# Moving small VectorE work between the matmul phases of a Strassen-Winograd feed-forward block

## The chip, the cores and the metric

The kernel runs on one core of a Trainium2 chip. The metric is device time in microseconds (us), the median of several executions. One further execution was recorded by the hardware profiler; all lines of profile below come from it. The engines are named as the profile names them: PE (TensorE, matmuls), PEld (its weight loads), DVE (VectorE), ACT (ScalarE), POOL (GpSimd) and SP (SyncE, which here only issues DMAs). Each engine works through its own queue in order; semaphores tie the queues together.

## The reference

32 sequences of 128 tokens with 512 features pass through a conditioned block. Its first half (layer norm, two small gelu networks) counts only for masked tokens; its second half is a feed-forward network for all tokens. In a short form:

```python
emb = silu(t) @ ada_w + ada_b                        # shift, scale, gate of the first half
norm = where(m, layernorm(x) * (1 + scale) + shift, 0)
x = x + gate * where(m, ssm(norm) + ssm_of_the_flipped(norm), 0)
shift2, scale2, gate2 = split(silu(t) @ ffada_w + ffada_b, 3)
ff = layernorm(x) * (1 + scale2) + shift2
h = gelu(ff @ ff_w1 + ff_b1)                         # 512 -> 1024
return x + gate2 * (h @ ff_w2 + ff_b2)               # 1024 -> 512
```

## The kernel before

The first 84 us compute the conditioning, the first half for the few masked tokens, and the layer norm of the first eight sequences. The rest, which the change is about, is the feed-forward network. It runs over four **pairs** (p = 0 to 3) of two sides of four sequences each, so 1024 tokens a pair.

**First product.** `ff @ ff_w1` is done with seven block products in place of eight (the Strassen-Winograd scheme), and each of these seven is again cut into seven. The outer seven are called **streams**, and run in the order 1, 2, 5, 6, 3, 7, 4 (`STREAMS`). Each has seven inner products P1 to P7. The text writes 6P3 for product P3 of stream 6. Such a **phase** is four matmuls of 128x128 by 128x256 on line 1117; P5, P2 and P3 add into the PSUM bank that the profile calls `e_m`, P1, P6, P7 and P4 into `a_m`.

After a phase, another engine does something that a later phase of the same stream has to wait for, because the inner sums are formed in PSUM between the matmuls:

- after P1, the **seed**: DVE L1161 `e_m<-a_m,ha` (in streams 1 and 5 an ACT copy, L1163). P2 waits for it.
- after P6, DVE L1142 `e_m<-a_m,...`. P3 waits for it.
- after P7, DVE L1147 `hb<-a_m,...`, which empties the bank. P4 waits for it.
- after P4, DVE L1152 (or ACT L1175). Nothing close waits for it.
- after P5, an ACT copy (L1131), and for streams with a predecessor two POOL additions `with_p5` (L1168), 128x512 each, into SBUF tiles `ha` and `hb`; stream 6 adds three more POOL additions (L1197, `after`), streams 7 and 4 some of L1201 (`late_sum`). L1142 and L1147 read what these leave.

A **window** (function `window`, new stream, old stream) interleaves two streams so that the waits are hidden: new P5, new P1, old P3, old P7, new P2, new P6, old P4. A dictionary `fills[w][n]` says what else is put in after step n of window w; `put(w, n, f, ...)` enters it. Window 1 is streams 2/1, window 2 is 5/2, window 3 is 6/5, window 4 is 3/6, window 5 is 7/3, window 6 is 4/7. All five compute queues stand in the order in which this program text runs (`manual_schedule`); no scheduler reorders them. A step therefore is put in a queue just where the text puts it.

**Sums of x.** The inputs of the streams are sums of blocks of x, made by DVE with `token_sums(j, n)`. j = 1 (L1046) makes the input of stream 5; j = 2 (L1050, tile `xn_sy`) that of stream 6; j = 3 (L1053) that of stream 7; j = 4 (L1056) that of stream 3. n names the part: n = 0 is read by P5 and P6, n = 1 by P1 and P2, n = 2 by P7 and P4 (each 128x512), and n = 3 by P3 (128x256). The text writes sum 4.1 for `token_sums(4, 1)`. Later sums read earlier ones, so their order on DVE is fixed. All their operands lie in SBUF.

**Other fills.** `take_first_half` puts gathers on POOL (L885, `DMA_INDIRECT`), which fetch rows of the first half's result for the next pair. `Statistics.one` is a bn_stats and a bn_aggr on DVE (L917, L918) for one tile of the next pair, `root` the reciprocal square root (L922 on DVE, L923 on POOL). `blocks(side, i)` normalises one such tile (DVE L929) and turns it in 32x32 blocks (DVE STREAM_TRANSPOSE). `fb2_step` is the difference of the two halves of a bias (DVE, 128x256), read by ACT L1243 when a bank of the second product is seeded. `fw2_of.combine` (L394) forms weight sums once, in pair 0.

**Second product.** `h @ ff_w2` follows with one level of the same scheme: 14 steps of 16 matmuls on line 1304. Its first two steps (P1U, P5U) and the third (P1V) stand between the last phases of stream 4; `first_block` (DVE L1251) makes the inputs of P5U and P5V. While it runs, DVE, ACT and DMA queues prepare the next pair, and the last steps are interleaved with stream 1 of the next pair.

Pair 0 is the special one: its first stream starts right behind the first half, so its sums of x come late, and window 1 is written out by hand ahead of the loop.

Of the kernel before, what the change touches and what calls it, by code (L numbers as in the profile page):

```python
# [22 lines left out]
def kernel(  # L23
# [49 lines left out]
    nc = tc.nc  # L73
# [503 lines left out]
    for key, vec in (("ssm1", ssm_b1), ("bwd1", bwd_b1), ("ff1", ff_b1)):  # L577
        n = vec.shape[0] // P
# [823 lines left out]
    now = FirstProduct(0, of_x[0].cut(), of_w)  # L1402
# [17 lines left out]
    for n in range(2, 4):  # L1420
        now.token_sums(1, n)
    now.do(2, "P2", "P6")
    for n in range(4):
        now.token_sums(2, n)
    now.do(1, "P4")
    now.token_sums(3, 0)
    for p in range(NP):
        more_pairs = p + 1 < NP
        xs = x_of[p]
# [2 lines left out]
        def put(w, n, f, *args):  # L1432
            fills.setdefault(w, {}).setdefault(n, []).append(lambda: f(*args))

        if p:
            for n, at in enumerate(((1, 3), (1, 4), (1, 6))):
                put(*at, now.token_sums, 2, 1 + n)
            put(1, 6, now.token_sums, 3, 0)
        for n, at in enumerate(((2, 1), (2, 3), (2, 3))):
            put(*at, now.token_sums, 3, 1 + n)  # L1440
        for n, at in enumerate(((2, 4), (2, 4), (2, 6), (2, 6) if more_pairs else (3, 1))):
            put(*at, now.token_sums, 4, n)
        put(3, 6, now.load_weights, 3)
        if p == 0:
            put(3, 6, load_rows_of_fw2, 0)
# [5 lines left out]
        second = SecondProduct(p, now.h, xs)  # L1451
        if p == 0:
            put(
                2, 0, nc.vector.tensor_tensor,
                fb2_step, fb2[:, D // 2 :], fb2[:, : D // 2], ALU.subtract,
            )
        put(6, 0, now.late_gelu, "11")
# [7 lines left out]
        if more_pairs:  # L1465
            x_next = x_of[p + 1]
            stats = [Statistics(x_next[side], f"{p + 1}_{side}") for side in range(2)]
            xn, xT = {}, {}

            def blocks(side, i):  # L1470

                if i == 0:
                    xn[side] = in_turned_blocks(
                        group_of_tiles(f"{p + 1}_0")
                        if side == 0
                        else sp.tile([P, G, D], F32, tag="s12", name=f"xn_{p + 1}_1")
                    )
                t = stats[side].normalised(i, xn[side][:, :, i])
                nc.vector.transpose(t, t)

            def to_feature_rows(side, *queues):
                xT[side] = new_xT(p + 1, side)
                turned(xn[side], xT[side], queues)

            if p:
                put(1, 6, take_first_half, p + 1, x_next, range(G))
            put(2, 6, take_first_half, p + 1, x_next, range(G, G + 2))
            put(3, 4, take_first_half, p + 1, x_next, range(G + 2, G + 3))
            put(5, 4, take_first_half, p + 1, x_next, range(G + 3, 2 * G))
            for i, at in enumerate(((3, 1), (3, 3), (3, 4), (3, 6))):  # L1490
                put(*at, stats[0].one, i)
            put(*((3, 6) if p else (5, 4)), stats[0].root)
            for i, at in enumerate(((4, 4), (4, 6), (5, 3), (6, 4))):
                put(*at, stats[1].one, i)
            put(6, 4, stats[1].root)
        for w in range(1 + (p == 0), 7):
# [2 lines left out]
        second.step(0)  # L1499
        now.late_gelu("21")  # L1500
        if more_pairs:
            for i in range(2):
                blocks(0, i)
        now.do(4, "P3")
        second.seed(1)
        now.do(4, "P7")
        second.first_block(1, 2, 4)
        if more_pairs:
            blocks(0, 2)
# [16 lines left out]
        if more_pairs:  # L1526

            for i in range(G):
                put(2 + i // 2, blocks, 1, i)
            for k in range(KC):  # L1530
                put(4 + k // 2, lambda k: scaled(2 * (p + 1), xT[0], k), k)
                put(7 + k // 2, lambda k: scaled(2 * (p + 1) + 1, xT[1], k), k)
                if k == 1:
                    put(4, to_feature_rows, 1, nc.sync, nc.sync, nc.sync, nc.scalar)

            def begin(j):
                if j == 1:
                    of_x[p + 1] = TokenBlocks(p + 1, (xT[0], xT[1]))
                of_x[p + 1].one(j)

            put(8, begin, 1)
            put(9, begin, 2)
            put(9, begin, 3)
            put(10, begin, 4)

            def next_product():
                nxt["p"] = FirstProduct(p + 1, of_x[p + 1].cut(), of_w)
                nxt["p"].load_weights(1)

            nxt = {}  # L1550
            put(10, next_product)
            put(11, lambda: nxt["p"].do(1, "P5", "P1"))
            for n in range(4):
                put(11 + n // 2, lambda n: nxt["p"].token_sums(1, n), n)
            put(13, lambda: nxt["p"].token_sums(2, 0))
            if p + 2 < NP:
                x_of[p + 2] = [[], []]
                put(11, lambda: x_of[p + 2][0].extend(load_side(p + 2, 0)))
            put(12, lambda: nxt["p"].do(1, "P2", "P6"))
            put(13, lambda: nxt["p"].load_weights(2))  # L1560
            if p + 2 < NP:
                put(13, lambda: x_of[p + 2][1].extend(load_side(p + 2, 1)))
# [128 lines left out]
```

## Time and profile before

| what | value |
|---|---|
| median of three runs | 456.78 us (456.37 to 456.99) |
| profiled execution, whole / span | 455.45 / 453.7 us |
| granted TensorE clock, mean | 0.999 |
| DVE busy | 331.7 us, 73% of the span |
| ACT, POOL busy | 178.0 and 159.8 us |
| share of PE in the chain that ended last | 92% |
| HBM traffic | 155 GB/s over the span |

The span is what the profiler saw from first to last instruction; the run is 1.7 us longer. In the 40 slices of the page, PE is at 9 tenths or more in every slice but the first and the last, so the profile has to be read at the level of single phases: the start times of neighbouring phases on PE tell where it waited. On an undisturbed stretch the phases of line 1117 start 0.863 us apart.

### The profile page before, as it was taken

The numbers are of one execution on the slowest core, as the hardware profiler recorded it, in microseconds if no ns is written. First come the engines' busy times: TensorE is split into PE (matmuls) and PEld (weight loads), VectorE is DVE, ScalarE is ACT, GpSimd is POOL, SyncE is SP. The second block draws the span as 40 slices with busy tenths as digits, with TensorE's granted clock in tenths as the row PEclk, the third lists the DMA queues.
The fourth block names the chain that finished last, engine by engine and source line by source line (L and its number), as shares of the span: only waits on it lengthen the run. The fifth ranks groups of instructions, "written<-read, shape, count | busy, mean of one in ns | idle before, by whom it ended". The sixth has DMA issues, their size and how long they took to land.

```text
span 453.7 us, 6170 instructions
## 1 busy us (share of the span) xinstructions
PE 446.6 (98%) x2151; PEld 370.4 (82%) x2151; DVE 331.7 (73%) x571; ACT 178.0 (39%) x390; POOL 159.8 (35%) x154
## 2 busy tenths in 40 slices
PE   8999999999999999999999999999999999999996
PEld 3884585688888888888888888888888888888885
DVE  5798797697789759886796498867963995534645
ACT  3124127244642552446425514454355154552000
POOL 4220550089770000797700007977000027560000
PEclk9999999999999999999999999999999999999999
DMA  7999449745518817722187167221872442222023
GB/s 251 379 396 407 150 73 326 279 151 172 189 78 180 114 49 251 249 92 82 66 191 107 56 230 264 95 84 54 202 105 59 157 145 82 81 94 93 0 82 107
DMA packets 82611, 70.57 MB, mean 156 GB/s; under 512 B 63112, under 2 KB 63728, under 8 KB 81554
## 3 DMA queue, kind: packets, MB, share of 16 engines
q1 hardware_dynamic: 67762, 58.28, 40.9%
q0 software_dynamic: 4160, 10.54, 6.9%
q10 hardware_dynamic: 10656, 1.33, 2.1%
q8 instruction: 18, 0.29, 0.2%
q14 instruction: 15, 0.12, 0.1%
HBM read 56.46 MB, written 13.70 MB: 155 GB/s over the span
## 4 chain that ended last, share of the span: by engine, by line
PE 92%; DVE 5%; POOL 1%; issue 1%; ACT 1%; DVEq 0%
PE a_o L1304 23%; PE a_m L1117 18%; PE e_o L1304 18%; PE e_m L1117 14%; PE po_s L221 6%; PE ph_s L204 5%; PE ph_s L673 2%; PE pm_ss L309 1%; PE last L1304 1%; PE pm_f L309 1%; PE a_m_alone L1117 1%; PE pl_s L254 1%; DVE xn_sy L1050 0%; PE part_s L333 0%; DVE e_m L1142 0%
## 5 line engine op out<-in xcount | busy, mean ns | idle before, releaser
L1168 POOL TENSOR_TENSOR ha<-p_m,ha 128x512 f32<-128x512 f32 x20 | 25.8, 1289 | 178.8 <-ACT ha L1175 169.2
L1304 PE MATMUL e_o<-fw,ha 128*128 128x256 f32 x256 | 57.9, 379 | 0.0
L939 ACT ACTIVATE xT<-xT,modT 128x128 f32<-128x128 f32 x112 | 44.1, 480 | 31.6 <-DMA xT<-xn 31.4
L1304 PE MATMUL a_o<-t,hb 128*128 128x256 f32 x240 | 54.1, 379 | 0.0
L1304 PEld LDWEIGHTS e_o<-fw,ha 128*128 128x128 f32 x256 | 48.6, 190 | 6.6
L1304 PEld LDWEIGHTS a_o<-t,hb 128*128 128x128 f32 x240 | 45.6, 190 | 6.2
L1079 ACT ACTIVATE hb<-hb,biasT 128x256 f32<-128x256 f32 x64 | 29.0, 500 | 30.4 <-POOL hb L1201 19.8
L1131 ACT COPY p_m<-e_m 128x512 f32<-128x512 f32 x27 | 15.8, 586 | 47.8 <-PE e_m L1117 43.3
L885 POOL DMA_INDIRECT x<-x_rows,slot_i x24 | 29.2, 1218 | 6.0 <-issue 5.3
L1168 POOL TENSOR_TENSOR hb<-p_m,hb 128x512 f32<-128x512 f32 x20 | 29.6, 1481 | 0.3
L1304 PE MATMUL a_o<-fw,ha 128*128 128x256 f32 x128 | 28.9, 379 | 0.0
L1304 PE MATMUL a_o<-t,s 128*128 128x256 f32 x128 | 28.9, 379 | 0.0
L1304 PE MATMUL e_o<-fw,s 128*128 128x256 f32 x128 | 28.9, 379 | 0.0
L221 PE MATMUL po_s<-w,h_s 128*128 128x512 f32 x64 | 28.4, 594 | 0.0
L1175 ACT COPY ha<-e_m 128x512 f32<-128x512 f32 x32 | 18.5, 578 | 24.9 <-PE e_m L1117 24.6
L1304 PEld LDWEIGHTS a_o<-t,s 128*128 128x128 f32 x128 | 24.3, 190 | 3.3
L1304 PEld LDWEIGHTS a_o<-fw,ha 128*128 128x128 f32 x128 | 24.3, 190 | 3.3
L1304 PEld LDWEIGHTS e_o<-fw,s 128*128 128x128 f32 x128 | 24.3, 190 | 3.3
L1142 DVE TENSOR_TENSOR e_m<-a_m,ha 128x512 f32<-128x512 f32 x20 | 13.9, 696 | 17.0 <-POOL ha L1168 6.6
L1079 ACT ACTIVATE ha<-e_m,biasT 128x256 f32<-128x256 f32 x48 | 20.0, 468 | 14.8 <-PE e_m L1117 12.6
L1117 PE MATMUL a_m<-xT,tw 128*128 128x256 f32 x96 | 24.7, 380 | 0.4 <-DVE hb L1147 0.4
L1117 PE MATMUL e_m<-s,fw 128*128 128x256 f32 x92 | 23.8, 381 | 0.0
(237 smaller groups left out, 892.3 us busy)
## 6 DMA issues: line engine op xcount, KB each, us to landing
tw<-t_rows SPq DMA_DIRECT2D x16, 896.0 KB, 5.3
x<-in_x_dram SPq DMA_DIRECT2D x16, 512.0 KB, 8.8
gate<-gate_rows POOLq DMA_DIRECT2D x8, 1024.0 KB, 5.2
out_dram<-x SPq DMA_DIRECT2D x15, 512.0 KB, 4.9
xT<-xn SPq DMA_DIRECT2D x92, 64.0 KB, 2.4
ada_f<-in_L_cond_ffada_w_dram SPq DMA_DIRECT2D x4, 768.0 KB, 13.2
ada_a<-in_L_cond_ada_w_dram SPq DMA_DIRECT2D x4, 512.0 KB
w<-in_L_cond_ssm_w_dram SPq DMA_DIRECT2D x2, 1024.0 KB, 6.2
```

What stands on the lines that cost most here:

```text
L204: nc.tensor.matmul(ph[:, :n], w[:, k, ts(f, P)], xT[:, k, :], start=(k == 0), stop=(k == KC - 1))
L221: nc.tensor.matmul(po, h[f][:, ts(i, P)], w[:, f, :], start=(f == 0 and seeded is None), stop=(f == HC - 1), skip_group_check=seeded is no ...
L309: nc.tensor.matmul(pm[ts(j, B), : (hi - lo) * P], sT[:, k, :], kinds[:, k, lo:hi, ts(j, P)], start=False, stop=True, skip_group_check=True,)
L885: nc.gpsimd.indirect_dma_start(out=xs[i // G][i % G // 2][:, i % 2], out_offset=None, in_=x1_rows, in_offset=bass.IndirectOffsetOnAxis(ap= ...
L939: nc.scalar.activation(out, src, AF.Identity, bias=shift, scale=scale)
L1079: nc.scalar.activation(dst[:, n], src[:, n], AF.Gelu_apprx_tanh, bias=biasT[:, f : f + 1])
L1117: nc.tensor.matmul(bank[:, ts(n, QT)], self.w_block(j, product)[:, ts(n, P)], self.x_block(j, product), start=(product in ("P1", "P5") and ...
L1131: nc.scalar.copy(p5, e)
L1142: nc.vector.tensor_tensor(e, a, p5, add)
L1168: nc.gpsimd.tensor_tensor(self.place(RESULT[j], c), self.p5[j], other, ALU.add)
L1175: nc.scalar.copy(self.place(RESULT[j], c), src)
L1304: nc.tensor.matmul(part, src[:, k, ts(i, P)], w[product][:, k, :], start=(last and k == 0), stop=True, skip_group_check=True,)
```

## The change

```diff
     now.do(2, "P2", "P6")
-    for n in range(4):
+    for n in range(2):
         now.token_sums(2, n)
     now.do(1, "P4")
-    now.token_sums(3, 0)
     for p in range(NP):
...
+        sums = [(j, n) for j in (2, 3, 4) for n in range(4)]
         if p:
-            for n, at in enumerate(((1, 3), (1, 4), (1, 6))):
-                put(*at, now.token_sums, 2, 1 + n)
-            put(1, 6, now.token_sums, 3, 0)
-        for n, at in enumerate(((2, 1), (2, 3), (2, 3))):
-            put(*at, now.token_sums, 3, 1 + n)
-        for n, at in enumerate(((2, 4), (2, 4), (2, 6), (2, 6) if more_pairs else (3, 1))):
-            put(*at, now.token_sums, 4, n)
+            at_sums = (
+                (1, 1), (1, 3), (1, 4), (1, 6), (1, 6), (2, 1), (2, 3), (2, 3),
+                (2, 4), (2, 4), (2, 6), (2, 6) if more_pairs else (3, 1),
+            )
+        else:
+            sums = sums[2:]
+            at_sums = (
+                (2, 1), (2, 3), (2, 3), (2, 4), (2, 4), (2, 6), (3, 1), (3, 1), (3, 3), (3, 3),
+            )
+        for at, of in zip(at_sums, sums):
+            put(*at, now.token_sums, *of)
...
         if p == 0:
             put(
-                2, 0, nc.vector.tensor_tensor,
+                4, 1, nc.vector.tensor_tensor,
                 fb2_step, fb2[:, D // 2 :], fb2[:, : D // 2], ALU.subtract,
             )
...
-            for i, at in enumerate(((3, 1), (3, 3), (3, 4), (3, 6))):
+            for i, at in enumerate(((3, 1), (3, 3), (3, 4), (4, 1)) if p else ((3, 4), (3, 6), (4, 1), (4, 3))):
                 put(*at, stats[0].one, i)
-            put(*((3, 6) if p else (5, 4)), stats[0].root)
-            for i, at in enumerate(((4, 4), (4, 6), (5, 3), (6, 4))):
+            put(*((4, 1) if p else (5, 4)), stats[0].root)
+            for i, at in enumerate(((4, 4), (5, 1), (5, 3), (6, 4))):
                 put(*at, stats[1].one, i)
             put(6, 4, stats[1].root)
...
         if more_pairs:
-            for i in range(2):
+            for i in range(1 + (p > 0)):
                 blocks(0, i)
         now.do(4, "P3")
         second.seed(1)
         now.do(4, "P7")
+        if more_pairs and p == 0:
+            blocks(0, 1)
         second.first_block(1, 2, 4)
...
             for n in range(4):
                 put(11 + n // 2, lambda n: nxt["p"].token_sums(1, n), n)
-            put(13, lambda: nxt["p"].token_sums(2, 0))
```

No instruction is added or taken away; nothing changes on PE, ACT and SP. On DVE the order changes in these places:

- Pair 0, windows 2 to 4. The last two of the sums 2.n, all of 3.n and 4.n, and `fb2_step` stand later. L1147 of 2P7 now comes ahead of sum 2.3 and the sums 3.n; the sums 4.n stand behind the seed of 6P1, two ahead of and two behind L1147 of 5P7. The first four bn_stats and `fb2_step` follow behind those.
- Pair 0, last phases. L1147 of 4P7 stands ahead of the second normalised tile and its transpose.
- Pairs 1 to 3. Sum 2.0 stands behind the seed of 2P1 and no longer ahead of it.
- Pairs 1 and 2. The fourth bn_stats and its root stand behind the seed of 3P1, another bn_stats behind the seed of 7P1 (the latter in pair 0 too).

On POOL, the reciprocal root of side 0 in pairs 1 and 2 moves behind the two L1168 of stream 3.

## The prediction

> **What bounds the kernel now.** I read the busy shares first:
>
> ```profile
> PE 446.6 (98%) x2151; PEld 370.4 (82%) x2151; DVE 331.7 (73%) x571; ACT 178.0 (39%) x390; POOL 159.8 (35%) x154
> ```
>
> PE sets the time, so a move on DVE is worth only the PE wait that it ends or makes. Next the timeline of PE. An undisturbed phase starts 0.863 us after the one before it (100.83 after 99.97 below).
>
> ```profile
> 97.75 1.03 PE L1117 MATMUL a_m<-sx,tw 128*128 128x256 f32 x4
> 99.00 1.13 PE L1117 MATMUL a_m<-xT,t 128*128 128x256 f32 x4 [0.23 <-DVE hb L1147]
> 99.97 1.03 PE L1117 MATMUL e_m<-xn_sy,tw 128*128 128x256 f32 x4
> 100.83 1.03 PE L1117 MATMUL a_m<-xn_sy,tw 128*128 128x256 f32 x4
> 101.75 1.13 PE L1117 MATMUL e_m<-sx,tw 128*128 128x256 f32 x4
> 102.72 1.03 PE L1117 MATMUL a_m<-sx,tw 128*128 128x256 f32 x4
> 103.88 1.13 PE L1117 MATMUL e_m<-xn_sy,tw 128*128 128x256 f32 x4
> 104.85 1.03 PE L1117 MATMUL a_m<-xn_sy,tw 128*128 128x256 f32 x4
> ...
> 129.89 3.62 PE L1304 MATMUL e_o<-fw,s 128*128 128x256 f32 x16
> 133.93 1.13 PE L1117 MATMUL a_m<-xT,tw 128*128 128x256 f32 x4 [0.42 <-DVE hb L1147]
> ```
>
> These are 5P6, 2P4 (99.00), 6P5, 6P1, 5P3 (101.75), 5P7, 6P2 (103.88), 6P6; then P5U and 4P4. A phase that had to wait costs its lateness plus 0.10, since the next starts 0.97 later and not 0.86. 2P4: 1.25 - 0.86 + 0.10 = 0.50. 5P3: 0.05 + 0.10 = 0.16. 6P2: 0.30 + 0.10 = 0.41. 4P4: 16 matmuls take 3.45, so 134.04 less 0.10 was due at 133.34; 0.59 + 0.10 = 0.69. Read the same way, 7P2 waits in pairs 1 and 2 (207.63, 298.58; 0.28 each) and 2P2 in pair 3 (365.35; 0.29). All these are 2.61 us. The rest of the network has next to no gap.
>
> Last, POOL and DVE, to see what stands in each other's way:
>
> ```profile
> 90.84 1.26 POOL L1168 TENSOR_TENSOR ha<-p_m,ha 128x512 f32<-128x512 f32 x1 [27.17 <-ACT ha L1175]
> 92.08 1.71 POOL L1168 TENSOR_TENSOR hb<-p_m,hb 128x512 f32<-128x512 f32 x1
> ...
> 98.59 1.00 POOL L885 DMA_INDIRECT x<-x_rows,slot_i  x1 [0.31 <-issue]
> 99.89 2.07 POOL L885 DMA_INDIRECT x<-x_rows,slot_i  x1 [0.30 <-issue]
> 102.26 1.83 POOL L885 DMA_INDIRECT x<-x_rows,slot_i  x1 [0.30 <-issue]
> 104.11 1.28 POOL L1168 TENSOR_TENSOR ha<-p_m,ha 128x512 f32<-128x512 f32 x1
> ```
>
> ```profile
> 91.65 1.01 DVE L1046 TENSOR_TENSOR sx<-xT 128x512 f32<-128x512 f32 x1
> 92.58 1.48 DVE L1046 TENSOR_TENSOR sx<-s 128x256 f32<-128x256 f32 x1
> ...
> 102.81 0.41 DVE L1056 TENSOR_TENSOR s<-s,xn_sy 128x256 f32<-128x256 f32 x1
> 103.14 0.68 DVE L1161 TENSOR_TENSOR e_m<-a_m,ha 128x512 f32<-128x512 f32 x1
> ```
>
> A sum whose operands all lie in SBUF and a POOL addition don't run together. The sum of 91.65 (0.68 elsewhere) ends at 92.66, 0.55 after the addition; the next addition ends 1.13 after that sum, at 93.79; the 256-wide sum, 0.41 elsewhere, ends 0.28 later still. So they alternate: the waiting addition goes ahead of the next sum. At 184.5, 275.4 and 366.4 the same rows show the same ends to 0.01. L1142, L1147, L1161 (PSUM operands) and bn_stats overlap additions with no loss. The point: before, the last sum ends at 103.2, ahead of the first addition of stream 6 at 104.11.
>
> **What goes.** 2P4's wait: L1147 loses sums 2.3, 3.0, `fb2_step` and 3.1 ahead of it and starts when 2P7 ends (97.15, from 98.27). 5P3 and 6P2 start on time too: L1142 of 5P6 ends at 100.6 for a need at 101.2, the seed of 6P1 at 102.15 for 102.93. That is 1.07. 4P4: L1147 moves ahead of the second tile, whose 1.27 (131.28) is 0.74 of waiting for POOL's addition; it ends some 1.4 before 4P4 is due: 0.69. L1147 then fills that wait, so the last `first_block` behind it, which ended at 138.02, ends about 0.5 earlier; P5V, due at 138.51 and now 0.69 earlier, still has it by 0.3. 7P2 in pairs 1 and 2: its seed sat behind a bn_stats and bn_aggr (0.81), which now follow: 0.56. The root moved on POOL costs nothing: it still stands ahead of the addition L1197 that L1142 of 3P6 waits for (204.84), so that wait stays. Sum 2.0 behind the seed, pair 3: 0.60 off the seed, 0.29 won; in pairs 1 and 2 PE had no wait there. `fb2_step` (0.34) is read by ACT at 122.3, late enough. All edits: -2.61.
>
> **What comes.** I queue the changed order of pair 0 by the durations above (sums 0.60 start to start, 256-wide 0.335, bn pair 0.81, DVE starts 0.10 after a phase's last matmul, which ends 1.03 after its start).
> - DVE: 2.3 at 97.75, 3.0, 3.1, 3.2, L1142 99.89, L1152, 3.3 at 101.09, seed 6P1 101.47, 4.0 at 102.07, 4.1 due 102.67.
> - POOL's gathers: the one of 97.07 now meets no sum (1.00, was 1.21); the next starts 98.38 in sum 3.0 (till 98.69, 1.27), the next 99.95 (1.00, was 2.07), the last 101.26 in 3.3 (1.14). Stream 6's first addition comes at 102.40 instead of 104.11, in the middle of sum 4.0.
> - So 4.0 ends 102.75, addition 103.87, 4.1 104.42, L1147 of 5P7 104.34 to 105.03 (due 103.27). 5P4, due 104.66, starts at 105.09: 0.43 + 0.10.
> - Second addition 105.55, sum 4.2 106.10, third (L1197) 107.22, sum 4.3 107.50, bn 107.42 to 108.24, L1142 of 6P6 to 108.93. 6P3, due 107.79 after the first delay, starts 108.99: 1.20 + 0.10.
> - `fb2_step` meets the additions of stream 3 and ends 111.2; bn; L1147 of 6P7 111.9 to 112.6; 6P4 due 112.55: 0.10 + 0.10. From there DVE is ahead again, POOL's later additions (1.3 later) still end before L1142 of 7P6, which ACT holds.
>
> New: 0.53 + 1.30 + 0.20 = 2.03, call it 2.04. Sum: 2.04 - 2.61 = -0.57, a span of 453.16 from 453.73. The profiled execution is 455.45 in all, the median of the runs 1.33 more; the difference carries over: **456.2**.
>
> Bounds of what the trace doesn't show, which is who wins where a gather waits for a sum: it let a second sum pass twice in ten such rows (99.89, 102.26, both beginning under 0.1 into the sum), never when it began later. Mine begin 0.29 and 0.17 into one. If one slips by 0.6, the addition comes at 103.0, 4.1 is through, and the new waits are 6P3 0.77 and 6P4 0.36: sum -1.5. Delayed by 1.2: 6P3 0.30 and 3P3 0.50, sum -1.8. I take the row that holds for later beginnings.
>
> [...]
>
> **Rivals.**
> 1. The additions miss the sums, or only touch them: the gathers slip as bounded above, or POOL lets queued sums pass. For it: two gathers did slip. Against: in all six rows where an addition waits and more DVE work on SBUF is queued (92.08, 184.48, 219.12, 275.44, 310.08, 366.39), the addition went first. 455.3 with one slip, 454.9 with two, 454.2 with no new wait at all (-2.61).
> 2. Slower: POOL becomes the bound of pair 0. It idles no more than 0.3 at a time from 90.84 to 117.89, and every meeting adds up to 0.6. If seven sums cost it 0.6 each, the addition for 7P6 ends at 116.66 + 4.2 = 120.9, where L1142 has to start by 118.6 to keep 7P3: 2.3 + 0.1 more. 2.04 + 2.4 - 2.61 = +1.8: 458.6. It decides from an end at about 119.5, half a microsecond past what ACT's copies allow with my delays. Against it: queued as above, POOL is 1.3 late.
> 3. The change doesn't do what it says: each L1147 and seed named does move ahead in the changed order, so only sizes are open.
>
> **Chances.** Forecast (meeting as queued, or its near variants) 0.60, rival 1 0.33, rival 2 0.07. 0.2% is 0.91 us, about what a measurement can tell: faster means below 455.87. The forecast's own range, 455.7 to 456.7, crosses that line, about 0.05 of its 0.60. So faster 0.38, same 0.55, slower 0.07. Range: the forecast's, down to rival 1's two slips and some room, 454.7; up 0.3 over the forecast's, 457.0; outside are no new wait and rival 2.
>
> **What will show it.** Right: 2P4, 4P4, the three seeds with no gap; the gather of 99.9 near 1.0; stream 6's first L1168 near 102.4; sums 4.1 and 4.3 stretched to 1.7 and 1.5; gaps before 5P4 and 6P3. Wrong: sums 4.n at 0.68 and no gap in pair 0 (rival 1), or L1142 of 7P6 waiting for POOL L1168 (rival 2).

## The result, and the profile after

The changed kernel takes 460.08 us (median of ten runs, 456.63 to 461.15) against 456.40 for the kernel before (ten runs, 455.51 to 457.21): a ratio of 1.0075 [1.0054, 1.0097]. It is slower by 3.7 us, where 456.2, or 0.57 less than before, was forecast and "slower" had a chance of 0.07. Nine of the ten runs lie between 459.1 and 461.2; the one of 456.63 has a span of 454.9 and the higher clock (0.999); no trace of it is on record, so why it was spared is not known.

The profiled execution has a span of 459.4, from 453.7. The page's busy shares and its row of granted clock (40 slices):

```profile
PE 448.9 (98%) x2151; PEld 372.4 (81%) x2151; DVE 338.8 (74%) x571; ACT 178.2 (39%) x390; POOL 159.5 (35%) x154
```

```profile
PEclk9999999998999999999999999999999999999998
```

PE is busy for 2.3 us more with the same matmuls, and two slices have a clock below 0.9: the tenth, 103 to 115 us, and the last, where PE's matmuls have ended (455.0). The timeline of PE in the tenth, with the same phases as shown before:

```profile
98.13 1.03 PE L1117 MATMUL a_m<-sx,tw 128*128 128x256 f32 x4
99.00 1.03 PE L1117 MATMUL a_m<-xT,t 128*128 128x256 f32 x4
...
101.59 1.03 PE L1117 MATMUL e_m<-sx,tw 128*128 128x256 f32 x4
...
103.31 1.03 PE L1117 MATMUL e_m<-xn_sy,tw 128*128 128x256 f32 x4
104.18 1.03 PE L1117 MATMUL a_m<-xn_sy,tw 128*128 128x256 f32 x4
108.32 1.55 PE L1117 MATMUL a_m<-sx,tw 128*128 128x256 f32 x4 [3.12 <-DVE hb L1147]
109.67 1.91 PE L1117 MATMUL e_m<-s,fw 128*128 128x256 f32 x4
111.37 1.49 PE L1117 MATMUL a_m<-xT,fw 128*128 128x256 f32 x4
112.70 1.03 PE L1117 MATMUL e_m<-xn_sy,tw 128*128 128x256 f32 x4
...
116.56 1.13 PE L1117 MATMUL a_m<-xn_sy,tw 128*128 128x256 f32 x4 [0.25 <-DVE hb L1147]
```

2P4 (99.00), 5P3 (101.59) and 6P2 (103.31) start 0.86 after the phase ahead of them: these waits are gone. But 5P4 starts 4.14 after 6P6 and not 0.86 after it, and the three phases from 108.32 to 112.70 take 4.38 and not 2.59. What 5P4 waited for stands on DVE and POOL:

```profile
102.47 4.60 DVE L1056 TENSOR_TENSOR s<-s,xn_sy 128x512 f32<-128x512 f32 x1
106.99 0.68 DVE L1056 TENSOR_TENSOR xT<-xT,xn_sy 128x512 f32<-128x512 f32 x1
107.59 0.68 DVE L1147 TENSOR_TENSOR hb<-a_m,p_m 128x512 f32<-128x512 f32 x1
```

```profile
101.65 1.12 POOL L885 DMA_INDIRECT x<-x_rows,slot_i  x1 [0.30 <-ACT p_m L1131]
102.80 1.28 POOL L1168 TENSOR_TENSOR ha<-p_m,ha 128x512 f32<-128x512 f32 x1
104.02 1.27 POOL L1168 TENSOR_TENSOR hb<-p_m,hb 128x512 f32<-128x512 f32 x1
105.24 1.26 POOL L1197 TENSOR_TENSOR ha<-ha 128x512 f32<-128x512 f32 x1
106.66 1.30 POOL L885 DMA_INDIRECT x<-x_rows,slot_i  x1 [0.16 <-issue]
```

Sum 4.0, 0.68 elsewhere, is recorded for 4.60: it comes 0.33 before the first addition of stream 6, and waits not for one addition but for all three, which run undelayed at 1.26 to 1.28. It ends at 107.07, 0.57 after the last of them. Sum 4.1 and L1147 of 5P7 follow, and 5P4 with them.

The windows view of the same stretch (time, then busy time of PE, PEld, DVE, ACT and POOL, the granted clock, the DMA's share and GB/s):

```profile
104.00:108.30 4.30, 1.20 (x6) 0.72 (x4) 4.30 (x4) 0.59 (x1) 3.80 (x4) 1.00 0.00 0
108.30:110.00 1.70, 1.68 (x5) 1.45 (x6) 1.67 (x5) 0.09 (x1) 0.00 (x0) 0.68 0.08 20
110.00:112.50 2.50, 2.50 (x8) 1.94 (x8) 1.42 (x4) 1.08 (x2) 0.15 (x1) 0.54 0.64 181
```

PE did next to nothing for 3.1 us. It then ran some 3.4 us at half the clock: the granted clock is 0.50 all through 109.0 to 112.2 and 1.00 again from 112.4 (the 0.68 and 0.54 above are means that take in some full speed), and matmuls start 0.427 apart and not 0.216. The half clock adds 1.79 to the 3.28 by which 5P4 is late.

The balance, read by the distances between phase starts as the prediction reads them: 5P4 3.28; the halved clock behind it 1.79; 6P4 0.51; P1V, behind 4P4, 0.37; the fourth products of stream 6 in pairs 1 and 2 0.23 each; pair 3's 2P2 and 2P3 0.41; 7P5 in pair 3 1.03. Together 7.85, less the 2.61 of the old waits: +5.24. The two spans differ by 5.64 (459.37 and 453.73), of which 0.39 lies before 84 us, where nothing was moved.

### The profile page after: what moved, and what is told of

Same layout as the page of the kernel before. It is cut to its first block, busy times and chain, and to the rows that moved or that the text cites. A ratio compares the mean times of both kernels' runs of the same rounds, so it can differ in the third digit from the quotient of the medians.

```text
span 459.4 us, 6170 instructions
## 1 busy us (share of the span) xinstructions
PE 448.9 (98%) x2151; PEld 372.4 (81%) x2151; DVE 338.8 (74%) x571; ACT 178.2 (39%) x390; POOL 159.5 (35%) x154
## 3 DMA queue, kind: packets, MB, share of 16 engines
q10 hardware_dynamic: 10656, 1.33, 2.1%
## 4 chain that ended last, share of the span: by engine, by line
PE 91%; DVE 3%; issue 2%; POOL 2%; DMA 1%; ACT 1%; DVEq 0%
PE a_o L1304 23%; PE a_m L1117 18%; PE e_o L1304 17%; PE e_m L1117 14%; PE po_s L221 6%; PE ph_s L204 5%; PE ph_s L673 2%; DMA tw<-t_rows 1%; PE pm_ss L309 1%; PE last L1304 1%; PE a_m_alone L1117 1%; PE pm_f L309 1%; PE part_s L333 1%; POOL hb L1201 1%; PE pl_s L254 1%
## 5 line engine op out<-in xcount | busy, mean ns | idle before, releaser
L1168 POOL TENSOR_TENSOR ha<-p_m,ha 128x512 f32<-128x512 f32 x20 | 26.3, 1315 | 183.6 <-ACT ha L1175 169.3
L885 POOL DMA_INDIRECT x<-x_rows,slot_i x24 | 27.8, 1159 | 6.0 <-issue 5.0
L1168 POOL TENSOR_TENSOR hb<-p_m,hb 128x512 f32<-128x512 f32 x20 | 29.6, 1482 | 0.3
```

The costliest lines, as they stand in the source:

```text
L885: nc.gpsimd.indirect_dma_start(out=xs[i // G][i % G // 2][:, i % 2], out_offset=None, in_=x1_rows, in_offset=bass.IndirectOffsetOnAxis(ap= ...
L1168: nc.gpsimd.tensor_tensor(self.place(RESULT[j], c), self.p5[j], other, ALU.add)
```

## The experiments

Times are beside the kernel before on the same chip (medians 456.1 to 456.4). A time marked "one execution" has no spread and shows little by itself, since executions of the kernel before on one chip spread over 1.6 to 3.9 us; what such a run shows is its trace. A **row** of additions means POOL additions that follow each other at once; a sum that waits for such additions is called shut out. Notation as in the prediction; the numbers on spans and waits are from each run's own trace.

**1. Is the wait there again?** The changed kernel, unaltered.

> The changed kernel once more, unaltered. In its first profile DVE sum 4.0 of pair 0 took 4.60 us (0.68 elsewhere): it was dispatched in the tail of POOL's last gather, and three POOL additions ran ahead of it, none of them delayed. Theory S (starved): a sum dispatched in a gather with additions queued right behind it gets no turn until POOL's queue has a pause; the stretch of 3.5 to 4.6 and the wait of some 3 us before phase 5P4 come again in this profile. Rival A (they alternate, as I forecast, and the first profile was an accident): the sum takes about 1.0 and the wait is 0.4. Time: S 460, A 456.

460.86 (459.19 to 460.98), ratio 1.0087 [1.0054, 1.0121]. Sum 4.0 takes 4.59, over three additions of 1.26 to 1.28; 5P4 starts 3.27 late, and the clock is 0.50 from 106.9 to 113.6. So it isn't an accident of one execution.

**2. Where in the change does the loss sit?** Pair 0's sums, `fb2_step` and the first four statistics at the places of before; the rest stays changed.

```diff
-    for n in range(2):
+    for n in range(4):
         now.token_sums(2, n)
     now.do(1, "P4")
+    now.token_sums(3, 0)
...
-            sums = sums[2:]
+            sums = sums[5:]
             at_sums = (
-                (2, 1), (2, 3), (2, 3), (2, 4), (2, 4), (2, 6), (3, 1), (3, 1), (3, 3), (3, 3),
+                (2, 1), (2, 3), (2, 3), (2, 4), (2, 4), (2, 6), (2, 6),
...
-                4, 1, nc.vector.tensor_tensor,
+                2, 0, nc.vector.tensor_tensor,
...
-            for i, at in enumerate(((3, 1), (3, 3), (3, 4), (4, 1)) if p else ((3, 4), (3, 6), (4, 1), (4, 3))):
+            for i, at in enumerate(((3, 1), (3, 3), (3, 4), (4, 1)) if p else ((3, 1), (3, 3), (3, 4), (3, 6))):
```

> The changed kernel with pair 0's sums, its bias step and its first four bn_stats at their old places; the tile behind 4P7 and all edits of pairs 1 to 3 stay. Both theories: the sums run before the additions again, the old waits before 2P4, 5P3 and 6P2 (1.07) come back, none near 5P4, clock 1.00; 4P4's 0.69 stays won. Against the kernel before 0.7 to 1.2 us less (455.2 to 455.7), which puts the whole loss of the change on the place of these sums. If it stays near 460, the loss is elsewhere.

455.71, ratio 0.9990 [0.9973, 1.0007]. The three old waits are back (2P4, 5P3 and 6P2, 0.50, 0.15 and 0.41 by the same reading), the loss is gone. So the whole loss comes from the place of pair 0's sums and of what was moved with them (`fb2_step`, four statistics), and all other parts together are worth 0.1%, within what can be told from no change.

**3. Sums 4.0 and 4.1 two phases later.** A sum that doesn't start in the tail of a gather.

```diff
-                (2, 1), (2, 3), (2, 3), (2, 4), (2, 4), (2, 6), (3, 1), (3, 1), (3, 3), (3, 3),
+                (2, 1), (2, 3), (2, 3), (2, 4), (2, 4), (2, 6), (3, 3), (3, 3), (3, 3), (3, 3),
```

> The changed kernel with sums 4.0 and 4.1 of pair 0 put behind L1147 of 5P7 with 4.2 and 4.3. Gathers as in the changed kernel, but sum 4.0 is now dispatched about 1.3 us later, in the second addition. S: the four sums alternate with the additions, no sum over 1.8 us; 5P4 has no wait, 3P5 and 3P1 wait some 1 us in all for 4.0 and 4.1. Rival B: sum 4.0 is shut out until the third addition ends, 2.5 us or more. Rival D: 4.6.

456.92 (one execution). Sum 4.0 comes 0.10 into the second addition and takes 2.95: it waits for the second and the third and gets in when POOL comes to its gather. So the tail of the gather isn't needed for it. PE waits twice, 1.3 and 1.1; the mean clock of the span is 1.000.

**4. The last two gathers ahead of the additions left out in pair 0.** This run leaves out part of the work: two tiles of the next pair miss their first-half rows.

```diff
-            put(2, 6, take_first_half, p + 1, x_next, range(G, G + 2))
+            if p:
+                put(2, 6, take_first_half, p + 1, x_next, range(G, G + 2))
```

> The changed kernel without the two gathers that stand in POOL's queue ahead of stream 6's additions in pair 0 (two tiles of the next pair then miss the first half's rows for masked tokens). The additions then start as soon as ACT's copy is there, about 101.2, and sum 4.0 is dispatched at 102.1 in the middle of the first addition, with no gather near. S: it waits for one addition only, as the sums of stream 5 do, and takes about 1.0 to 1.3; the following sums alternate; PE's waits before 5P4 and 6P3 together are under 2 us and the clock stays at 1.00. Rival B (whatever the gathers do, three additions in a row shut a sum out): sum 4.0 takes 3 us or more. Rival D (it is the sum itself, not POOL): 4.6 again.

457.21 (one execution). POOL now rests 1.62 ahead of the first addition. Its timeline, and DVE's:

```profile
100.72 1.38 POOL L1168 TENSOR_TENSOR ha<-p_m,ha 128x512 f32<-128x512 f32 x1 [1.62 <-ACT p_m L1131]
102.06 1.72 POOL L1168 TENSOR_TENSOR hb<-p_m,hb 128x512 f32<-128x512 f32 x1
104.10 1.35 POOL L1197 TENSOR_TENSOR ha<-ha 128x512 f32<-128x512 f32 x1 [0.33 <-ACT ha L1175]
```

```profile
101.53 1.12 DVE L1056 TENSOR_TENSOR s<-s,xn_sy 128x512 f32<-128x512 f32 x1
102.57 1.75 DVE L1056 TENSOR_TENSOR xT<-xT,xn_sy 128x512 f32<-128x512 f32 x1
```

Here sums and additions do alternate: sum 4.0 gets in after one addition, the second addition is stretched to 1.72, sum 4.1 to 1.75. This is the picture that the prediction drew for the change. The waits left on PE are 0.9 and less. A little later `fb2_step`, begun 0.16 into the second addition of stream 3, also gets in after one, though POOL had rested only 0.84 ahead of that row:

```profile
107.74 1.26 POOL L1168 TENSOR_TENSOR ha<-p_m,ha 128x512 f32<-128x512 f32 x1 [0.84 <-ACT p_m L1131]
108.96 1.26 POOL L1168 TENSOR_TENSOR hb<-p_m,hb 128x512 f32<-128x512 f32 x1
110.19 1.45 POOL L1197 TENSOR_TENSOR ha<-ha 128x512 f32<-128x512 f32 x1
```

```profile
109.12 1.39 DVE L1432 TENSOR_TENSOR fb_step<-fb 128x256 f32<-128x256 f32 x1
```

**5. A gather ahead of the additions instead of behind them.** The additions start later, so another sum meets them.

```diff
-            put(3, 4, take_first_half, p + 1, x_next, range(G + 2, G + 3))
+            put(*((3, 4) if p else (2, 6)), take_first_half, p + 1, x_next, range(G + 2, G + 3))
```

> After the runs so far: a sum dispatched 0.1 into the second addition, more than a us after the gather's end, was shut out by two additions (2.95), while without the two gathers sums and additions alternated (1.12, 1.75). Theory S2: after a gather, as long as POOL goes on without a pause, a sum gets no turn until POOL pauses. Rival A2 (only a sum dispatched before or right at the start of an addition loses). Here the gather of step (3, 4) of pair 0 stands with the others at (2, 6), so the additions come some 1.3 later, at 103.7, right behind the last gather; sums 4.0 and 4.1 meet gatherings only and take 0.7 to 1.3. Sum 4.2, dispatched about 103.9: S2, it waits for all three additions, 3.3 to 4.0; A2, if it is dispatched before 103.8 the same, else one addition, 1.7. Time in both near 457; with S2 phase 6P3 waits 1.5 or more.

459.99 (one execution). Sums 4.0 and 4.1 pass in 0.68 and 0.74; sum 4.2, started 0.23 into the first of the additions, takes 4.05 while three of them run at 1.27 or 1.28. 6P3 comes 3.65 late, and the clock is 0.995 over the span. So it isn't sum 4.0 or its place: here it is sum 4.2 that meets the row. The row does not end there, though: a fourth addition follows without a rest, and this one waits for the sum.

```profile
106.58 1.27 POOL L1197 TENSOR_TENSOR ha<-ha 128x512 f32<-128x512 f32 x1
107.81 1.73 POOL L1168 TENSOR_TENSOR ha<-p_m,ha 128x512 f32<-128x512 f32 x1
```

**6. A short rest of POOL.** A one-element operation on POOL that waits for ACT's copy after 5P3 stands ahead of the three additions.

```diff
-                if prior and j not in (2, 4):
+                if prior and j not in (2, 4) and not (self.p == 0 and j == 6):
...
+            pause = stp.tile([1, 1], F32, tag="pause", name="pause", bufs=1)
+            put(
+                3, 2, nc.gpsimd.tensor_scalar,
+                pause, now.place("22", "12")[0:1, 0, 0:1], 1.0, None, ALU.add,
+            )
+            put(3, 2, now.with_p5, 6, "12")
+            put(3, 2, now.with_p5, 6, "22")
```

> The changed kernel with a pause in POOL's queue between the last gather and stream 6's additions in pair 0: a one-element POOL operation there reads ACT's copy after 5P3, which ends at about 102.9, and the two additions follow it; POOL idles from 102.4 to then. Sums 4.0 and 4.1 run in the pause, sums 4.2 and 4.3 (dispatched 103.9 on) meet additions. S2: the pause has ended POOL's hold, so sums and additions alternate: no sum over 1.8, some addition stretched to 1.4 to 1.8. Rival B2 (additions that stand close shut sums out whatever came before): sum 4.2 takes 2.5 or more and no addition is stretched. PE: no wait before 5P4 over 0.3; time 455 to 456 with S2.

456.80 (one execution). POOL rests 0.56, does the small operation, and adds; DVE's sum 4.2 is shut out by three again (104.05 3.82):

```profile
103.11 0.51 POOL L1432 TENSOR_SCALAR pause<-ha 1x1 f32<-1x1 f32 x1 [0.56 <-ACT ha L1175]
103.60 1.26 POOL L1168 TENSOR_TENSOR ha<-p_m,ha 128x512 f32<-128x512 f32 x1
104.83 1.26 POOL L1168 TENSOR_TENSOR hb<-p_m,hb 128x512 f32<-128x512 f32 x1
```

No gather stands directly ahead of the row, and the sum is shut out all the same. The clock makes a difference, too: 6P3 starts 2.29 late here and the clock stays at 1.00, and the total is 3 us under that of the changed kernel, for a wait that is 1.0 shorter (one execution, and not the only wait that differs).

**7. Sums earlier, the gather moved, the root in pairs 1 and 2 later.** A first attempt at a better version.

```diff
-                (2, 1), (2, 3), (2, 3), (2, 4), (2, 4), (2, 6), (3, 1), (3, 1), (3, 3), (3, 3),
+                (2, 1), (2, 1), (2, 1), (2, 3), (2, 3), (2, 4), (2, 4), (2, 6), (3, 1), (3, 1),
...
-            put(3, 4, take_first_half, p + 1, x_next, range(G + 2, G + 3))
+            put(*((3, 4) if p else (2, 6)), take_first_half, p + 1, x_next, range(G + 2, G + 3))
...
-            put(*((4, 1) if p else (5, 4)), stats[0].root)
+            put(5, 4, stats[0].root)
```

> A version that keeps what was won and avoids the meeting. Pair 0: sums 2.2, 2.3 and 3.0 in the gap ahead of L1147 of 2P7, 3.1 and 3.2 behind it, 3.3 and 4.0 ahead of L1142 of 5P6, 4.1 behind L1152 of 2P4, 4.2 and 4.3 behind the seed of 6P1; the gather of step (3, 4) stands at (2, 6), so that additions begin after about 103.4. The root of side 0 is put at (5, 4) in all pairs, so that its small DVE operation (1.09 in an addition in pair 1, ahead of L1147 of 6P7) is not ahead of a wait. All theories: no sum meets an addition, no PE wait over 0.2 in pair 0 before 4P4, where ACT's bank seed keeps some 0.4; in pairs 1 and 2 the waits before 6P4 (0.23) go. Against the kernel before 1.5 to 2.1 us less, 454.3 to 454.9.

458.52, ratio 1.0048 [1.0032, 1.0064]: a miss. The sums are through by 103.5, but a gather beside them takes 2.44, the additions start at 105.72, and six of them run in a row to 113.1. Now `fb2_step` meets them: 110.07, 3.30, shut out by three, 6P4 2.77 late, the clock halved again (0.994 over the span). The waits of pairs 1 and 2, however, are gone with the root's new place.

**8. A long rest of POOL.** The two L1168 of stream 6 are held back behind L1197, which waits for ACT's copy after 6P2; sums 4.2 and 4.3 stand behind a one-element operation of DVE that waits for the same copy.

```diff
-                if prior and j not in (2, 4):
+                if prior and j not in (2, 4) and not (self.p == 0 and j == 6):
...
-                (2, 1), (2, 3), (2, 3), (2, 4), (2, 4), (2, 6), (3, 1), (3, 1), (3, 3), (3, 3),
+                (2, 1), (2, 3), (2, 3), (2, 4), (2, 4), (2, 6), (3, 1), (3, 1), (3, 4), (3, 4),
...
+            late = stp.tile([1, 1], F32, tag="late", name="late", bufs=1)
+            put(
+                3, 4, nc.vector.tensor_scalar,
+                late, now.place("21", "11")[0:1, 0, 0:1], 1.0, None, ALU.add,
+            )
+            put(3, 4, now.with_p5, 6, "12")
+            put(3, 4, now.with_p5, 6, "22")
```

> The changed kernel with the three additions of stream 6 in pair 0 held back: the two L1168 are issued in 6P2 (behind L1197 of quarter 11, which waits for ACT's copy after 6P2, so POOL should be idle some 1.5 to 2.5 us behind the gathers), sums 4.2 and 4.3 stand in 6P2 too, behind a one-element DVE operation that waits for the same copy. So sum 4.2 is dispatched 0.1 to 0.5 into the first of three additions that could follow each other at once. Theory I (POOL's history decides: after a rest of 1.6 us or more a sum is let in after one addition, behind a run of gathers it is not): sum 4.2 takes 1.4 to 1.8, the addition after it is stretched to 1.6 to 1.8, no PE wait above 2. Theory D (the moment of dispatch decides: earlier than some 0.7 us into an undelayed addition means shut out until POOL stops adding): sum 4.2 takes 3.5 to 4.2, the three additions take 1.26 to 1.29 each, and PE waits over 2 us for 6P3 with a halved clock behind it. Total 457 to 458 by I, 459 to 460.5 by D.

460.25 (one execution). It did not test what it was made for: DVE got in first. What it showed, on POOL and on DVE:

```profile
104.20 2.16 POOL L1197 TENSOR_TENSOR ha<-ha 128x512 f32<-128x512 f32 x1 [2.28 <-ACT ha L1175]
...
110.00 1.28 POOL L1168 TENSOR_TENSOR ha<-p_m,ha 128x512 f32<-128x512 f32 x1
111.22 1.27 POOL L1168 TENSOR_TENSOR hb<-p_m,hb 128x512 f32<-128x512 f32 x1
112.45 1.27 POOL L1197 TENSOR_TENSOR ha<-ha 128x512 f32<-128x512 f32 x1
```

```profile
104.22 0.67 DVE L1056 TENSOR_TENSOR xT<-xT,xn_sy 128x512 f32<-128x512 f32 x1
104.81 0.41 DVE L1056 TENSOR_TENSOR s<-s,xn_sy 128x256 f32<-128x256 f32 x1
...
109.62 4.38 DVE L1432 TENSOR_TENSOR fb_step<-fb 128x256 f32<-128x256 f32 x1
```

Sum 4.2 starts 0.02 after L1197 and runs in 0.67; sum 4.3 follows it at once, and the addition, 1.27 elsewhere, waits for both (2.16). So two sums in a row can keep an addition out, as a row of additions keeps a sum out. Six microseconds later the roles are turned: `fb2_step`, 0.41 elsewhere, comes in the tail of a gather, 0.38 before the first of three additions, and takes 4.38. 6P4 waits 3.39 and starts at 115.47; the clock is 1.00 to 116.7 and 0.50 from 116.9 to 120.1. It is the failure of the changed kernel at another place, with another operand and half the width.

**9. The old places, and the root of pairs 1 and 2 later.** Experiment 2, and one line more.

```diff
-            put(*((4, 1) if p else (5, 4)), stats[0].root)
+            put(5, 4, stats[0].root)
```

> Pair 0's sums, the step of fb2 and the first four statistics at the places of before, the rest as changed, and L921/L922 (root and rstd) of pairs 1 and 2 four windows later at (5, 4), as pair 0 has them. Theory: the new waits before 6P4 of pairs 1 and 2 (0.12 and 0.10 behind it, twice) go and the old ones of 7P2 do not come back; with pair 3's as in sums_back 455.2 (454.6 to 455.7), ratio 0.997 or 0.998, no PE start over 0.30 us after the one before between 150 and 360. Rival: the root only moves its wait to another product, 455.7 and a ratio of 0.999.

455.24, ratio 0.9978 [0.9958, 0.9998]. No start on PE between 150 and 360 us is more than 0.24 after the one before: both the old wait before 7P2 and the new one before 6P4 are gone.

**10. Pair 0's sums forward instead of back.** In the kernel before DVE stands idle from 86.2 to 88.2 and from 89.0 to 89.7.

```diff
-    for n in range(2):
+    for n in range(4):
         now.token_sums(1, n)
+    now.token_sums(2, 0)
+    nc.vector.tensor_tensor(fb2_step, fb2[:, D // 2 :], fb2[:, : D // 2], ALU.subtract)
...
     now.do(2, "P5")
+    now.token_sums(2, 1)
     now.seed(2)
...
-    for n in range(2, 4):
-        now.token_sums(1, n)
     now.do(2, "P2", "P6")
-    for n in range(2):
+    for n in range(2, 4):
         now.token_sums(2, n)
     now.do(1, "P4")
+    now.token_sums(3, 0)
...
-            sums = sums[2:]
+            sums = sums[5:]
...
-                (2, 1), (2, 3), (2, 3), (2, 4), (2, 4), (2, 6), (3, 1), (3, 1), (3, 3), (3, 3),
+                (2, 1), (2, 3), (2, 3), (2, 4), (2, 4), (2, 6), (2, 6),
```

The statistics and the root are as in experiment 9, and the old `put` of `fb2_step` is gone.

> A version made from the findings: pair 0's sums go forward instead of back. Sums 1.2, 1.3, 2.0 and the step of fb2 in DVE's idle 86.1 to 88.1, sum 2.1 in the idle 88.8 to 89.5, 2.2 and 2.3 behind 2P6, the rest at the places of before; the statistics of pair 0 as before, the later ones spread as in the change; L921/L922 of every pair in 6P1's window after next (5, 4). Theory: DVE's queue runs 1 to 1.5 us ahead of before at 94 to 104, no addition meets a sum that waits, so the waits of 2P4 0.50, 5P3 0.16 and 6P2 0.41 are gone or under 0.1 each, with no wait above 0.5 in 104 to 120: 454.1 (453.3 to 455.0), ratio 0.995. Rival P (POOL bounds this stretch: six gathers, then three additions, cannot start earlier): L1142 of 6P6 or 3P6 waits for POOL what was won, 455.0, as v3. Rival S (a sum is shut out by two or three additions at another place): over 457 with a gap of 2.5 us or more.

455.16, ratio 0.9976 [0.9959, 0.9993]: no better than experiment 9, and short of the forecast. The waits of 2P4 and 5P3 are gone, but the gathers come earlier too, the first addition stands at 101.28, and the last sum, 4.3, meets it (1.49 for 0.41). The seed of 6P1 behind it is late, 6P2 loses 0.93 and 0.10.

**11. No sum left to meet.** Experiment 10 with the sums 3.2 to 4.3 one step further forward.

```diff
-                (2, 1), (2, 3), (2, 3), (2, 4), (2, 4), (2, 6), (2, 6),
+                (2, 1), (2, 1), (2, 1), (2, 3), (2, 3), (2, 4), (2, 4),
```

> v2_sums_in_idle with its sums 3.2 and 3.3 put where DVE stood idle (95.7 to 97.1, in 2P7's place the window before) and sums 4.0 to 4.3 one or two products earlier, so that all of pair 0's sums are done by 100 and none is left when the first addition of stream 6 starts at about 101.5. Theory (the meeting of a sum with an addition is all that is left to pay in this stretch): sum 4.3, which waited there for one addition (1.49 instead of 0.41) and held the seed L1161 and PE back (1.144 between two starts at 103.55, 0.93 and 0.10 lost), takes 0.41; no PE start over 0.30 us after the one before between 90 and 130; the three additions of stream 6 take 1.26 to 1.33; 454.1 (453.3 to 454.9), ratio 0.995 or 0.996. Rival: the sums press on the six gathers instead (2.0 or more for one, as in v1), the additions start after 103 and L1142 of 6P6 waits for POOL: 455.2, as v2, with a gap of 0.5 or more near 106.

454.12 (452.85 to 455.19), ratio 0.9953 [0.9935, 0.9971]; the span is 451.8. This beats both kernels. The row of additions starts with no sum near it (the last ends at 99.45):

```profile
101.64 1.28 POOL L1168 TENSOR_TENSOR ha<-p_m,ha 128x512 f32<-128x512 f32 x1
102.87 1.28 POOL L1168 TENSOR_TENSOR hb<-p_m,hb 128x512 f32<-128x512 f32 x1
104.12 1.27 POOL L1197 TENSOR_TENSOR ha<-ha 128x512 f32<-128x512 f32 x1
```

No start on PE between 90 and 130 us comes more than 0.24 after the one before.

**12. One sum back into the row.** Experiment 11 with the last sum, 4.3 (128x256), behind the seed of 6P1.

```diff
-                (2, 1), (2, 1), (2, 1), (2, 3), (2, 3), (2, 4), (2, 4),
+                (2, 1), (2, 1), (2, 1), (2, 3), (2, 3), (2, 4), (3, 1),
```

> v2b_no_meeting with a single sum moved by three products: 4.3 (128x256) from 5P2 to behind the seed of 6P1. DVE reaches it at about 101.6, POOL then ends its sixth gather and starts the first of three additions at 101.5 to 101.7 without a rest and without having waited for a sum. Theory (such an addition and those behind it keep the sum out; it gets in when POOL stops adding): sum 4.3 takes 3.8 to 4.4, the three additions 1.26 to 1.33 each, L1147 of 5P7 ends some 3.5 later than in v2b, PE waits 3 or more for 5P4 and its clock halves behind that: 458 to 459.5, ratio to before 1.004 to 1.008, for one sum of 0.41. Rival (as I forecast for the change: the sum waits for one addition only): 4.3 takes 1.4 to 1.6, the second addition 1.4 to 1.7, 5P4 late by 1 or less, 455 to 455.4.

455.57, ratio 0.9994 [0.9978, 1.0010]: 1.4 us more than experiment 11 (the spans are 453.2 and 451.8). On DVE, POOL and PE:

```profile
101.88 2.65 DVE L1056 TENSOR_TENSOR s<-s,xn_sy 128x256 f32<-128x256 f32 x1
```

```profile
101.75 1.27 POOL L1168 TENSOR_TENSOR ha<-p_m,ha 128x512 f32<-128x512 f32 x1
102.97 1.26 POOL L1168 TENSOR_TENSOR hb<-p_m,hb 128x512 f32<-128x512 f32 x1
104.45 1.27 POOL L1197 TENSOR_TENSOR ha<-ha 128x512 f32<-128x512 f32 x1 [0.21 <-ACT ha L1175]
```

```profile
105.98 1.13 PE L1117 MATMUL a_m<-sx,tw 128*128 128x256 f32 x4 [1.37 <-DVE hb L1147]
```

The mechanism is as expected and the size is not (458 to 459.5 was expected; the time of the rival, 455 to 455.4, is nearer): both L1168 run undelayed past the waiting sum, but L1197 then waits 0.21 for ACT, and in that gap the sum gets in. As it is shut out by two and not by three, 5P4 waits 1.37, and the phases behind it start 0.97 and 0.86 apart, as at the full clock. One sum of 0.41, moved by three products, takes back 1.4 of the 2.1 that experiment 11 had won. Read by phase starts, 5P4 costs 1.64; the spans differ by 1.43, because 0.33 more lies before 84 us and the wait of 7P5 in pair 3 (below) is 0.54 shorter here.

**The meetings together.** The table has sums and `fb2_step` against rows of additions. "Ahead" is what POOL did before the row of additions; the start is the sum's, against the addition that it meets.

| Sum (experiment) | Ahead of the row | Start | Additions waited for | Took, us |
|---|---|---|---|---|
| 4.0 (changed kernel) | gather, no rest | 0.33 before the first | 3 | 4.60 |
| 4.0 (3) | gather, no rest | 0.10 into the second | 2 | 2.95 |
| 4.2 (5) | gather, no rest | 0.23 into the first | 3, then a fourth waits for it | 4.05 |
| 4.2 (6) | rest 0.56, small operation | 0.45 into the first | 3 | 3.82 |
| `fb2_step` (7) | gather, then three additions | 0.68 into the fourth | 3 | 3.30 |
| `fb2_step` (8) | gather, no rest | 0.38 before the first | 3 | 4.38 |
| 4.3 (12) | gather, no rest | 0.13 into the first | 2, then POOL rests 0.21 | 2.65 |
| 1.2 (before) | rest 27.17 | 0.81 into the first | 1 | 1.01 |
| 4.0 (4) | rest 1.62 | 0.81 into the first | 1 | 1.12 |
| `fb2_step` (changed kernel) | rest 4.39 | 0.04 into the second | 1 | 1.50 |
| `fb2_step` (4) | rest 0.84 | 0.16 into the second | 1 | 1.39 |
| 4.3 (10) | gather, but the first addition itself waited for a sum (1.33) | 0.11 into the first | 1 | 1.49 |

A sum got in after one addition where POOL had rested for 0.84 us or more ahead of the row, or where that addition had itself waited for a sum. Where the row came straight behind other work, or behind a rest of 0.56 and a small operation, it stayed out for two or three additions. It then got in mostly where POOL rested or went over to a gather, but in experiment 5 ahead of a fourth addition, so it need not wait for the whole row. The moment of the start does not order the rows: 0.04 and 0.16 into an undelayed addition got in after one, 0.68 did not. The nearest to a matched pair is sum 4.3 in experiments 10 and 12, at 0.11 and 0.13 into the first addition. So what POOL did before orders the table; what decides it inside the chip is not shown by any of these runs, and the one made for it (8) did not reach its case.

## Why the prediction was wrong

**What goes** held in part. 2P4, 5P3 and 6P2 start on time, 1.06 where 1.07 was forecast. 4P4's wait goes too, but of the 0.69 only 0.32 is kept, for P1V behind it waits for its weights, and those for a bank that ACT seeds:

```profile
138.74 0.59 ACT L1243 COPY a_o<-fb 128x512 f32<-128x512 f32 x1
```

```profile
139.38 1.59 PEld L1304 LDWEIGHTS a_o<-fw,ha 128*128 128x128 f32 x8 [0.51 <-ACT a_o L1243]
```

The step named DVE's work behind 4P4 and forgot ACT's queue. 7P2 in pairs 1 and 2 starts on time, but "the root moved costs nothing" is wrong: its L922, 0.34 before, now stands ahead of L1147 of 6P7, starts inside an addition and takes 1.09. That gives back 0.23 of 0.28, twice; experiment 9 shows that a later place has neither wait. In pair 3 the 0.29 is lost again at 2P2 and 2P3 (0.17 and 0.24): sum 2.0, behind the seed, now meets the L1168 of 369.65, which takes 1.74.

**What comes: the gathers** held to 0.02. They take 1.00, 1.26, 1.00 and 1.12 where 1.00, 1.27, 1.00 and 1.14 were queued, and the first L1168 of stream 6 stands at 102.80, or 102.41 without the 0.39 of the start, where 102.40 was queued. Gathers begun inside a sum mostly took longer than the 1.00 of one that met none: 1.26 inside sum 3.0 here, 2.44 in experiment 7, 2.07 and 1.83 in the trace of before. One in experiment 5, begun 0.01 into sum 4.1, took 1.00, and that sum 0.74.

**What comes: the meeting** is the step that failed: "So 4.0 ends 102.75, addition 103.87, 4.1 104.42". Sum 4.0 was taken to be in ahead of the addition, and every later sum to wait for one addition. Sum 4.0 waited for three. The rows that "they alternate" was read from (91.65 and its three like) all stand behind a POOL that had rested 27 us or more; the row in question stands behind six gathers. The trace of before had no meeting of that sort, and the text named as unknown only who wins between a gather and a sum. The bound for a sum against a row of additions was missing: one addition on the one side, the whole row, 3 x 1.23, on the other. With it, rival 2 would have had a place and a price: 5P4 late by 3.3 instead of 0.43. Why sum 4.0, which starts 0.33 ahead of the first addition, is passed by it stays open.

**The clock** is the other half, and was in no rival. Of the 5.07 lost at 103 to 113 us, 1.79 is the halved clock. PE stood idle for 3.12 here, 3.11 in experiment 1, 2.61 in 7, 3.39 in 8 and 3.49 in 5, and in each of these five traces a stretch at a granted clock of 0.50 came with it: of some 3.4 us in four of them, and of 6.8 in experiment 1. Behind 2.13 (6), 1.42 (8), 1.37 (12) and 1.15 (3) the clock stayed at 1.00. The stretch does not begin at a fixed distance from the wait: in experiment 1 the clock is 0.50 from 106.9, ahead of 5P4's start at 107.50, in 8 it falls more than 1.2 after 6P4's start. Behind PE's last matmul, where nothing is left to slow down, it falls some 2.1 after the matmul's end in the changed kernel (457.1) and some 3.1 in the kernel before (452.5). Of the executions without a trace, one of three in experiment 1 and five of seven in experiment 7 have a mean clock of 0.998 or more, against 0.991 to 0.995 in the others; what PE waited in them is not recorded. In these traces waits of 2.61 and more between phases came with a halved clock and those of 2.13 and less did not; where the bound lies, and whether a wait of 2.13 at another moment would have come with one, no run shows.

**Rivals.** Rival 1 (the additions miss the sums) did not happen in the changed kernel, but its price was right for a kernel in which it does: with no new wait it put 454.2, and experiment 11, where no sum meets the row, gave 454.12. That they agree so closely is in part luck: rival 1 took 2.61 from 456.78, experiment 11 is 2.09 under the 456.21 beside it, and it also has the root at a later place and 0.86 of waiting at 7P5 in pair 3. Rival 2 (slower, 458.6) had the sign and a size 1.5 short, by a mechanism that did not occur: POOL was not late through many small meetings, since the three additions of stream 6 lost nothing. Forecast 6P3 1.30 and 6P4 0.20: 6P3 has no wait, since 5P4's delay covers it, and 6P4 has 0.51.

That the loss comes from the sums' place is shown by experiment 2; that a wait for several additions makes it, by experiments 5, 8, 11 and 12.

## What to carry to other kernels

Where operations of two engines hold each other up, as the sums and the additions do here (0.68 for a 512-wide sum alone, 1.01 to 4.60 in a meeting), a wait seen once is a sample of one history: price a new meeting from one operation up to the row that stands behind it on the other engine (three additions were the most that a sum waited for here), and look at what that engine did just before. Work that nothing waits for belongs into idle time ahead of such a row, not behind it: the same sums, with what was moved beside them, cost 4.4 us moved back (460.08 against 455.71 in experiment 2) and won 1.1 moved forward until none met the row (454.12 against 455.24 in experiment 9). And a wait on PE can have two prices: in the traces of these runs a stretch at half the clock came with every wait between phases of 2.6 us or more, and in the changed kernel it cost 1.79.

## What else the runs showed

In pair 3, 7P5 waits for its weights from DRAM (L1063) in ten of the thirteen traces of changed kernels, and not in the kernel before. Its start is late by 0.96 in the changed kernel, 1.07 in experiment 1, 0.72 in 3, 0.52 in 6, 1.15 in 7, 0.96 in 10, 0.78 in 11, and 0.14 to 0.28 in 4, 5 and 12 (0.07 to 0.08 more is lost behind it, hence the 1.03 of the balance); it isn't late in 2, 8 and 9. The transfer is issued at the same point each time. What differs in the records is one 16 KB packet near it, of the queue kind that the profile calls instruction: it took 0.92 to 0.93 in before, 2 and 9, and 1.5 to 2.4 in the ten that wait, though also 2.0 in experiment 8, which does not. There may be a link; no run was made for it.

A small DVE operation can wait as well: L922, on 128x4 elements, took 1.09 inside an addition in pairs 1 and 2, and 0.34 and 0.33 at its place in the kernel before.
